# Filler products of the identity in the planned idle of TensorE, and the conditioning padded to 128 columns

## Chip, cores and metric

The kernel runs on one core of a Trainium2 chip. The metric is device time in microseconds; the time before is the median of three runs, 1363.4 us (1363.39 to 1395.84).

## What is computed

Sixteen sequences `b` of 256 positions and 256 channels pass through two blocks, all in float32. The reference, cut:

```python
m = silu(cond) @ w_ada + b_ada            # cond is [16, 256]; nine chunks of 256 columns
h = _ln(x) * (1 + sc_msa) + sh_msa
x = x + self_attn(h) * g_msa              # 16 heads, rolled windows of 128
h = _ln(x) * (1 + sc_mca) + sh_mca
x = x + topk_cross_attn(h, ctx) * g_mca   # the 16 largest scores of each row are kept
h = _ln(x) * (1 + sc_mlp) + sh_mlp
x = x + swiglu(h) * g_mlp
...
# second block: _ada_ln of x and of ctx with silu(cond) @ Wss + bss, then cross attention
return x_q + (out @ Wp + bp)
```

Every shift and scale is thus a product of a 256-column slice of `w_ada` or `Wss` with the conditioning of all 16 sequences. It is made once, near the start, and used for all of them.

## The kernel before

All work is declared through `plan.op(engine, cost, emit, reads, writes, ...)`. `Plan.order()` sorts the operations by a due time from the table `DUE` (in units of one sequence) and their number, and that is the order in which every engine's instructions are written out. No cost enters the sort. `order()` then walks this list with the planned costs (`cost`, `hold`, `SWITCH`, `LAG`, and for DMAs `ISSUE`, `BEGIN`, `LAND`, `RATE`, `OPEN`) and gives each operation a planned start and end. This walk decides one thing in the program: which of the equal buffers of a kind (eight PSUM banks of the kind `W`, five `prT`, and so on) an operation takes, namely the one that the walk sees free first. `run()` then calls each operation's `emit` in that order.

TensorE's steps that matter here, by the line of the matmul:

- `ada_columns` (L703): for one shift or scale, four calls of `matmul` with a 128x128 slice of weights as the stationary operand and `condT[:, c, :]`, 16 columns, as the moving one. A float32 call makes two MATMUL records (a transpose makes one), so this is eight records. There are ten such operations, two for each of five norms; they are planned at 1.7 us each. `conditioned` makes `condT` (DVE L688), `out_of_it` (DVE L709, L711) adds the bias.
- `gate_rows` (L744): `condT[:, c, :]` as the stationary operand, 256 moving columns.
- `product` (L475), `values` (L511), `projected` (L558) and the feed-forward (L888, L915): 256 moving columns, 128x128 stationary.
- `four` (L780 and L788 for self attention, L827 for the top-k scores, L932 and L944 for the last attention): four calls that sit in the four groups of 32 rows. L827 has 512 moving columns in each call.
- `weighted` (L581): probabilities times values, in the four groups of 32 columns. `turned` (L449) and `probs_turned` (L525): transposes.

A top-k round is L827, then for each of its four banks on VectorE `MAX8` (L846), two `MATCH_REPLACE8` (L854), `MAX8` (L866) and two more `MATCH_REPLACE8` (L871); ScalarE makes the exponentials (L859), GpSimd multiplies (L875), TensorE transposes the product (L525). `self_attention` puts its row maxima into `q2` by sixteen tiny DMAs on SP's queue (`lower`, L605, eight for each half of the heads) before L788 runs. After each residual add GpSimd and VectorE normalize (L399, L425 to L437), TensorE turns (L449), and the next product follows.

The order of the start: sequence 0's self attention (planned and run up to about 50 us), its normalization and query product, its first top-k round, into which sequence 1's self attention and the rest of the weights are worked; from sequence 2 on, the stages of three sequences interleave. The last sequence is worked in two halves of 128 positions, with little beside them.

## Time and profile before

| | |
|---|---|
| median of the runs | 1363.4 us |
| the profiled execution's own time | 1365.2 us |
| its span, first to last instruction | 1363.1 us |
| mean granted TensorE clock | 0.981 |
| busy: TensorE, VectorE, GpSimd, ScalarE | 1327.1, 1216.9, 1026.4, 1014.4 us |
| chain that ended last, TensorE's share | 87% |

A timeline row gives start, duration from the first start to the last end of the merged instructions, engine, line, operation, shapes and count; in brackets stands the engine's idle time before it and what released it. The length of a run of matmuls is better read from its start to the next row's start, since the last one's drain overlaps what follows. The clock of a stretch is the granted share of TensorE's full rate.

### The profile page before, as it was taken

To read this page: it belongs to the slowest core of one execution; us is meant where nothing else is said; L and a number is where in the kernel's file an instruction comes from. 1 tells how busy PE (TensorE), PEld (TensorE's weight loads), DVE (VectorE), ACT (ScalarE), POOL (GpSimd) and SP (SyncE) were. 2 spreads that over 40 slices of the span, in tenths; PEclk is the share of its full clock that TensorE was granted. 3 is DMA by queue.
4 is the path that set the end of the run, shared out by engine and by line. 5 is a ranking of instruction groups with operands and counts; after the bars stand their busy time and mean duration, and the time that the engine had idled before them with its cause. 6 is when DMAs were issued, how large, how long until landed. Compare 5 with 4: busy or idle time off the path is not lost.

```text
span 1363.1 us, 38514 instructions
## 1 busy us (share of the span) xinstructions
PE 1327.1 (97%) x13464; PEld 1040.8 (76%) x13464; DVE 1216.9 (89%) x4357; ACT 1014.4 (74%) x2359; POOL 1026.4 (75%) x1552
## 2 busy tenths in 40 slices
PE   8699999999999999999999999999999999999996
PEld 6466787878778787877878787787878777787875
DVE  3699999999999999999999999999999999998734
ACT  4256778877777878777787878778787877877773
POOL 2456887878788787878878787787878787878752
PEclk9788999999999999999999999999999999999998
DMA  5412000101000010100001010001101000000000
GB/s 158 147 53 58 18 25 18 40 18 41 16 20 25 19 40 18 41 17 18 25 22 37 17 41 18 18 25 22 36 18 41 25 18 25 26 2 10 10 2 18
DMA packets 64161, 42.44 MB, mean 31 GB/s; under 512 B 37764, under 2 KB 56752, under 8 KB 63712
## 3 DMA queue, kind: packets, MB, share of 16 engines
q1 hardware_dynamic: 63967, 39.99, 10.9%
q8 instruction: 107, 1.75, 0.5%
q14 instruction: 87, 0.70, 0.2%
HBM read 35.14 MB, written 4.29 MB: 29 GB/s over the span
## 4 chain that ended last, share of the span: by engine, by line
PE 87%; DVE 5%; POOL 2%; DMA 2%; SPq 1%; issue 1%; ACT 1%; ACTq 0%; POOLq 0%; DVEq 0%
PE W L888 17%; PE W L475 11%; PE W L581 11%; PE W L525 8%; PE W L915 7%; PE W L511 6%; PE W L558 6%; PE W L944 5%; PE W L932 5%; PE W L827 5%; PE W L449 3%; PE W L788 3%; PE W L780 2%; DVE rest L854 1%; DVE rest L871 1%
## 5 line engine op out<-in xcount | busy, mean ns | idle before, releaser
L875 POOL TENSOR_TENSOR prT<-rest,prT 128x512 f32<-128x512 f32 x256 | 325.7, 1273 | 63.5 <-DVE rest L871 49.8
L859 ACT ACTIVATE prT<-W,ntop 128x256 f32<-128x256 f32 x512 | 216.8, 510 | 76.0 <-POOL ntop L848 64.3
L588 DVE TENSOR_REDUCE nm<-W 128x2 f32<-128x512 f32 (+1 forms) x384 | 236.9, 681 | 28.1 <-PE W L932 16.0
L888 PE MATMUL W<-xT,w_L_xcond_w_m 128*128 128x256 f32 (+1 forms) x1088 | 249.0, 375 | 1.5 <-ACT xT L463 1.5
L612 ACT ACTIVATE pTO<-W 128x512 f32<-128x512 f32 (+1 forms) x392 | 200.5, 613 | 62.0 <-PE W L944 37.6
L888 PEld LDWEIGHTS W<-xT,w_L_xcond_w_m 128*128 128x128 f32 x1088 | 189.1, 190 | 57.0 <-ACT pTO L612 10.9
L854 DVE MATCH_REPLACE8 rest<-top,W 128x256 f32<-128x256 f32 x512 | 208.2, 416 | 0.2 <-issue 0.2
L871 DVE MATCH_REPLACE8 rest<-top,rest 128x256 f32<-128x256 f32 x512 | 205.5, 409 | 0.0
L846 DVE MAX8 top<-W 128x8 f32<-128x256 f32 x512 | 187.0, 417 | 14.7 <-PE W L827 14.5
L866 DVE MAX8 top<-rest 128x8 f32<-128x256 f32 x512 | 187.3, 410 | 0.0
L525 PE MATMUL W<-ident,prT 128*128 128x128 f32 x1024 | 144.4, 279 | 11.1 <-POOL prT L875 11.1
L528 ACT ACTIVATE pTT<-W 128x512 f32<-128x512 f32 x256 | 148.4, 621 | 8.8 <-PE W L525 8.7
L541 POOL TENSOR_TENSOR on<-tr,rec 128x128 f32<-128x128 f32 (+1 forms) x162 | 71.0, 443 | 98.6 <-DVE rec L540 98.2
L525 PEld LDWEIGHTS W<-ident,prT 128*128 128x128 f32 x1024 | 120.3, 143 | 32.6 <-POOL prT L875 14.6
L905 POOL TENSOR_TENSOR mb<-ma,mb 128x256 f32<-128x256 f32 (+1 forms) x136 | 94.7, 697 | 62.7 <-ACT mb L903 50.6
L538 DVE STREAM_TRANSPOSE tr<-W 128x256 f32<-128x256 f32 (+1 forms) x162 | 79.2, 490 | 48.1 <-PE W L581 40.1
L915 PE MATMUL W<-w_L_xcond_w_m,h 128*128 128x256 f32 x512 | 113.8, 380 | 0.0
L581 PE MATMUL W<-pTO,v 128*32 128x128 f32 (+1 forms) x2112 | 108.1, 329 | 2.3 <-ACT pTO L612 2.0
L915 PEld LDWEIGHTS W<-w_L_xcond_w_m,h 128*128 128x128 f32 x512 | 95.9, 190 | 13.6 <-POOL prT L875 0.8
L908 POOL TENSOR_TENSOR h<-h,mb 128x256 f32<-128x256 f32 (+1 forms) x136 | 94.8, 697 | 8.3
L581 PEld LDWEIGHTS W<-pTO,v 128*32 128x32 f32 x2112 | 57.8, 111 | 42.6 <-ACT h L907 10.2
L903 ACT ACTIVATE mb<-W,half 128x256 f32<-128x256 f32 (+1 forms) x136 | 69.6, 513 | 9.7 <-PE W L888 8.4
(126 smaller groups left out, 2675.2 us busy)
## 6 DMA issues: line engine op xcount, KB each, us to landing
gate<-gates SPq DMA_DIRECT2D x48, 256.0 KB
q<-nmT SPq DMA_DIRECT2D x480, 1.0 KB
cx<-in_ctx_dram SPq DMA_DIRECT2D x19, 256.0 KB
cx<-in_ctx_dram SPq DMA_DIRECT2D x104, 32.0 KB
rest<-in_L_xcond_w_ada_dram SPq DMA_DIRECT2D x9, 256.0 KB
x<-in_x_dram SPq DMA_DIRECT2D x16, 128.0 KB
x<-in_x_dram SPq DMA_DIRECT2D x32, 64.0 KB
w_L_xcond_w_m<-in_L_xcond_w_m_dram SPq DMA_DIRECT2D x1, 2048.0 KB
```

Source lines behind the costliest of these rows:

```text
L525: nc.tensor.transpose(w.t[:, ts(n, P)], flat[:, ts(n, P)], ident)
L581: nc.tensor.matmul(po.t[ds(NW * j, NW), ds(q0, nq)], v.t[:, kt, 8 * m + 2 * j + a, :], pT.t.rearrange("p n q -> p (n q)")[:, ds(part, nq)] ...
L588: op("DVE", 0.61, lambda j=j, s=s: nc.vector.tensor_reduce(nm.t[:, k, ds(j, groups, step=4)], s.t.rearrange("p (g k) -> p g k", g=groups), ...
L612: op("ACT", 0.24 + q * 0.0005, lambda s=s, pT=pT: nc.scalar.activation(pT.t.rearrange("p n q -> p (n q)")[:, :q], s.t[:, :q], AF.Exp), r=[ ...
L846: nc.vector.max(top.t[:, a, 0:8], s.t[:, ts(a, L)])
L854: nc.vector.match_replace(rest.t[:, a, :], top.t[:, a, 0:8], s.t[:, ts(a, L)], TAKEN)
L859: nc.scalar.activation(pr.t[:, a, :], s.t[:, ts(a, L)], AF.Exp, bias=ntop.t[:, a:a + 1])
L866: nc.vector.max(top.t[:, a, 8:16], rest.t[:, a, :])
L871: nc.vector.match_replace(rest.t[:, a, :], top.t[:, a, 8:16], rest.t[:, a, :], TAKEN)
L875: op("POOL", 1.25, lambda: nc.gpsimd.tensor_tensor(pr.t, rest.t, pr.t, ALU.mult), r=[rest, pr], w=[pr])
L888: nc.tensor.matmul(w.t[:, :q], w_m1.t[:, c, ds(n0, P)], xT.t[:, c, :q], start=c == 0, stop=c == NCC - 1)
L915: nc.tensor.matmul(pp.t[:, ts(k, C)], hs[f].t[:, ts(k, P)], w_m2.t[:, f, :], start=f == 0, stop=f == NHC - 1)
```

## The change

`order()` looks at every TensorE operation whose planned start is more than `IDLE` = 0.8 us after the planned end of the one before it. If a PSUM bank was free by that end plus 0.3 us, it notes `n = int((gap - 0.3) / FILLER)` fillers, with `FILLER` = 0.43 us, for the bank freed last among these, and books the bank until the operation starts. `run()` writes the fillers out just ahead of the operation. A filler is a float32 matmul of the 128x128 identity with the identity repeated four times, 512 moving columns, whose result nobody reads. Two planned DMA constants change, `ISSUE` from 0.47 to 0.53 and `LAND` from 1.0 to 0.4.

`condT` becomes 128 columns for each of its two chunks, the last 112 zero (one memset), and `ada_columns` multiplies all 128 and uses the first 16; it is now planned at 0.9 us instead of 1.7. `gate_rows` takes the first 16 columns as before.

```diff
-ISSUE, BEGIN, LAND, RATE, OPEN = 0.47, 0.9, 1.0, 320.0, 8
+
+IDLE, FILLER = 0.8, 0.43
+ISSUE, BEGIN, LAND, RATE, OPEN = 0.53, 0.9, 0.4, 320.0, 8
...
             o.start = t
+            if o.eng == "PE" and t - free["PE"] > IDLE and free["PE"]:
+
+                n = int((t - free["PE"] - 0.3) / FILLER)
+                ok = [z for z in slots["W"] if z[0] < free["PE"] + 0.3]
+                if ok and n:
+                    at, slot = ok[-1]
+                    slots["W"].remove((at, slot))
+                    insort(slots["W"], (t, slot))
+                    o.fill = self.tiles["W"][slot], n
...
+            if o.fill:
+                self.filler(*o.fill)
             o.emit()
...
+    def filler(t, n):
+        for _ in range(n):
+            nc.tensor.matmul(t, ident, ident.unsqueeze(1).to_broadcast([P, 4, P]), start=True, stop=True)
+    plan.filler = filler
...
-    condT = fixed("condT", [P, NCC, B])
+    condT = fixed("condT", [P, NCC, P])
+    nc.vector.memset(condT.t, 0.0)
...
-        op("DVE", 0.2, lambda: nc.vector.tensor_copy(condT.t.rearrange("p c b -> p (c b)"), w.t[:, :NCC * B]), r=[w], w=[condT])
+        op("DVE", 0.2, lambda: nc.vector.tensor_copy(condT.t[:, :, :B], w.t[:, :NCC * B].rearrange("p (c b) -> p c b", c=NCC)), r=[w], w=[condT])
...
-                    nc.tensor.matmul(pm.t[:, ts(m, B)], w.t[:, c, ts(m, P)], condT.t[:, c, :], start=c == 0, stop=c == NCC - 1)
-        op("PE", 1.7, emit, r=[w, condT], w=[pm], mode=128)
+                    nc.tensor.matmul(pm.t[:, ts(m, P)], w.t[:, c, ts(m, P)], condT.t[:, c, :], start=c == 0, stop=c == NCC - 1)
+        op("PE", 0.9, emit, r=[w, condT], w=[pm], mode=128)
...
-                nc.tensor.matmul(pg.t[:B, :C], condT.t[:, c, :], w.t[:, c, :], start=c == 0, stop=c == NCC - 1)
+                nc.tensor.matmul(pg.t[:B, :C], condT.t[:, c, :B], w.t[:, c, :], start=c == 0, stop=c == NCC - 1)
```

The two lines of `out_of_it` read `pm.t[:, ds(m * P, B)]` instead of `pm.t[:, ts(m, B)]`.

More of the change, by code (lines that the diff above doesn't have):

```diff
@@ L181 @@
 class Op:
-    __slots__ = ("tag", "eng", "cost", "hold", "own", "kb", "emit", "due", "mode", "takes", "uses", "after", "start", "end", "n")
+    __slots__ = ("tag", "eng", "cost", "hold", "own", "kb", "emit", "due", "mode", "takes", "uses", "after", "start", "end", "n", "fill")
 class Plan:
@@ L200, in op @@
         o.eng, o.cost, o.emit, o.mode, o.n = eng, cost, emit, mode, len(self.ops)
-        o.tag = self.tag
+        o.tag, o.fill = self.tag, None
         o.after, o.takes, o.uses = {*after}, [], []
@@ L708, in out_of_it @@
                 if plus_one:
-                    nc.vector.tensor_scalar(dst.t[:, m, :], pm.t[:, ts(m, B)], col(bias, chunk + m), 1.0, ALU.add, ALU.add)
+                    nc.vector.tensor_scalar(dst.t[:, m, :], pm.t[:, ds(m * P, B)], col(bias, chunk + m), 1.0, ALU.add, ALU.add)
                 else:
-                    nc.vector.tensor_scalar(dst.t[:, m, :], pm.t[:, ts(m, B)], col(bias, chunk + m), None, ALU.add)
+                    nc.vector.tensor_scalar(dst.t[:, m, :], pm.t[:, ds(m * P, B)], col(bias, chunk + m), None, ALU.add)
         op("DVE", 0.32, out_of_it, r=[pm, cols(bias)], w=[dst])
```

## Prediction

> **What bounds the kernel now.** I read the page first: the busy shares, and the row of granted clock.

> ```profile
> span 1363.1 us, 38514 instructions
> ...
> PE 1327.1 (97%) x13464; PEld 1040.8 (76%) x13464; DVE 1216.9 (89%) x4357; ACT 1014.4 (74%) x2359; POOL 1026.4 (75%) x1552
> ...
> PEclk9788999999999999999999999999999999999998
> ```

> TensorE (PE) sets the pace; from about 140 us to 1280 us it is never idle and at full clock, and VectorE (DVE) is close behind. What this change can touch lies in the first three or four slices of 34 us and in the last two. So next the busy time by stretch, TensorE alone (columns: stretch and its length, busy time with count, granted clock, DMA share, GB/s).

> ```profile
> 31.00:32.00 1.00, 0.64 (x24) 1.00 0.15 33
> 32.00:33.00 1.00, 1.00 (x16) 0.71 0.02 2
> 40.00:44.00 4.00, 4.00 (x65) 0.50 1.01 290
> 46.00:47.00 1.00, 1.00 (x5) 0.96 0.97 385
> ...
> 62.00:64.00 2.00, 0.00 (x0) 0.79 0.03 6
> 74.00:78.00 4.00, 4.00 (x33) 0.50 0.02 6
> 80.00:81.00 1.00, 1.00 (x26) 0.89 0.00 0
> 98.00:100.00 2.00, 1.27 (x9) 1.00 0.04 13
> 100.00:102.00 2.00, 0.93 (x4) 0.67 0.59 166
> ```

> The clock falls to half three times: from 32.4 to 46.1, 63.2 to 80.2 and 100.7 to 110.9 us. It also reads 0.66 in two stretches of 5 us near the end (1335 to 1340, 1345 to 1350). Then the timeline of TensorE, and of VectorE, where the longest idle lies:

> ```profile
> 58.24 1.14 PE L827 MATMUL W<-k,q 32*128 32x512 f32 x8 [0.56 <-ACT q L486]
> 68.24 1.11 PE L525 MATMUL W<-ident,prT 128*128 128x128 f32 x4 [8.86 <-POOL prT L875]
> 69.29 2.09 PE L827 MATMUL W<-k,q 32*128 32x512 f32 x8
> 71.31 1.11 PE L525 MATMUL W<-ident,prT 128*128 128x128 f32 x4
> ...
> 84.65 1.14 PE L827 MATMUL W<-k,q 32*128 32x512 f32 x8
> 85.72 1.08 PE L581 MATMUL W<-pTO,v 128*32 128x128 f32 x32
> ```

> ```profile
> 69.57 0.75 DVE L866 MAX8 top<-rest 128x8 f32<-128x256 f32 x2
> 71.39 0.77 DVE L846 MAX8 top<-W 128x8 f32<-128x256 f32 x2 [1.08 <-PE W L827]
> ```

> TensorE waits 8.86 us for the first transposed probabilities while VectorE works off four banks; VectorE itself is out of work at 70.3 us and waits for the second L827. So here VectorE is the bound, and L827's place in TensorE's order feeds it.

> **What a filler costs.** The nearest rows: 16 records of 256 columns (L475) run from 23.99 to 27.44 us, 3.45 us, or 0.216 us a record and 0.43 us a call. A 512-column call has twice the columns: 0.86 us. L827 has 512 columns; its four calls sit beside each other in four row groups and take 85.72 - 84.65 = 1.07 us, some 0.2 of it for the change of mode, which leaves 0.87 for calls of that length. The planned 0.43 is therefore half. At half clock the first L475 records (16 in 5.14 us from 12.09, part cold) and L511 (8 in 3.49 us from 76.86, 0.87 a call of 256) give 1.7 us a filler. I take 0.86 with the clock up; 0.43 and 1.7 are the ends.

> **How many fillers, and where.** This is a count from the walk in `order()`, with the new constants put in by hand; the plan's times are not used as times. Gaps over 0.8 us with a bank free:

> - before the second L703, gap 1.07: 1; before the first L475 (waits for w_qkv), 1.77: 3;
> - the shorter L703 opens gaps before the first L788 (1.03: 1), before both L581 of sequence 0 (1.39: 2, 1.31: 2) and before the L449 of prep0 (1.51: 2); before the first L827, 1.13: 1;
> - before the L525 at 68.24, 9.01: 20;
> - in the end: before two L888 (1.20: 2, 1.33: 2), an L475 (1.20: 2), an L932 (1.18: 2), an L944 (0.90: 1), an L581 (1.34: 2) and the last L558 (1.89: 3).

> At the short gaps from 63.9 to 110 and at 1213 all banks are taken, so nothing goes in. That is 32 in front and 14 at the end, 46 calls or 92 records. No other engine's order, and no DMA of SP's queue or GpSimd's, is added or moved, since the sort knows no cost; buffers may rotate differently, which I put at nothing (bound 1 us either way).

> **Part by part.**

> *Padding.* Ten L703 steps of eight records. With 16 columns they take 0.92 us at full clock (49.00 to 49.92) and 1.73 cold (4.43 to 6.16): the weight loads set the pace (LDWEIGHTS 128x128, median 192 ns, overlapped). 128 columns stream in half of 0.216 us, 0.11 a record, 0.86 for eight. So padding costs nothing in itself (bound 0 to 0.2 us each, 2 in all). The memset of 256 columns lies in VectorE's idle ahead of 2.92 us (1.78 us, waiting for a DMA): nothing, 0.3 if that cover were gone. What it may bring is clock: in the 3.4 us before 32.4 TensorE ran 1.0 us of L703, two short L788 and only 0.36 us idle, and still fell to half. With 16 of 128 columns counted as work the rest was about 1.8 us; the stretch from 56.3 to 59.7 had 2.4 us and kept the clock. Padded it would be 2.8. I take it as kept.

> [...]

> *0 to 30 us.* The filler ahead of the second L703 (cold, 1.7 us for 0.2 idle) and three ahead of L475 (2.6 us for 1.6 idle) push L475 from 12.09 to about 14.5; having started warm it needs 3.45 instead of 5.3 us. Net +0.5 (+4 if the clock is still low then, -1 if neither waits).

> *30 to 58 us.* At full clock L788, L703, L581, L780 and L744 would save up to 6.8 us (13.6 us at half rate). SP's sixteen L605 (issued 25.5 to 35.6 at about 0.6 us) still hold the second L788 back to about 36.6, against 36.20 now, and ScalarE's four exponentials (2.06 us) follow; GpSimd's chain holds L558 to about 44.3 against 46.11. So -2, less 0.3 for the two fillers ahead of L449 and one ahead of L827: L827 ends near 57.6 instead of 59.4, -1.8 (bounds -3 and +3, the fillers without the clock).

> *58 to 140 us.* Twenty fillers last 17.2 us, from 57.6 to 74.8, where the probabilities are ready near 66.4. They write the bank whose reader (ACT q L486) is done, so they wait for nothing. L525 and the second L827 are behind them; L827 ends at 76.4 instead of 71.4. VectorE starts its second round +5.0 late: its 13 us of cover end 6.6 us too early. After that TensorE is at full clock where it was at half, which removes VectorE's 1.15 us wait for L581 at 81.56 and part of its 2.7 us idle from 110 to 140. TensorE's own balance is no worse (it has 7.9 us of cold loss and 6 us of idle to give from 71 to 140), but VectorE is busy over 90% there. Of +5 I leave +2 at 140 us; bounds -3 (TensorE's balance alone decides) and +7 (VectorE recovers nothing and the clock still dips at 100).

> *140 to 1280 us.* No filler, TensorE full, so the +2 is carried.

> *End.* The rows of the idle, each filler run charged by 0.86 less the idle there:

> ```profile
> 1307.88 3.07 PE L888 MATMUL W<-xT,w_L_xcond_w_m 128*128 128x128 f32 x24 [0.93 <-ACT xT L463]
> ...
> 1334.96 1.28 PE L475 MATMUL W<-xT,w_L_xcond_Wq 128*128 128x128 f32 x8 [0.55 <-ACT xT L463]
> 1336.79 3.44 PE L932 MATMUL W<-k,q 32*128 32x256 f32 x32 [0.55 <-ACT q L497]
> ```

> Two fillers are 1.7 us: +1.2 and +0.8 at the two L888 (idle 0.55 at 1291 and 0.93), +1.2 at L475, +1.2 at L932, +0.5 at L944, +0.4 at the last L581, which ScalarE holds anyway, +1.0 at the last L558 (2.6 us against 1.11 idle and a first half that had already run). All are on the chain of waits, and nothing after makes it good. The two stretches at 0.66 cost 3.4 us of TensorE; I take 1 us back. Sum +5 (bounds +2, +7).

> **Sum.** +2 and +5 give +7 on the span of 1363.1. The profiled execution took 1365.2 us, 2.1 over its span and 1.8 over the median; on the median this is 1363.4 + 7 = 1370.

> [...]

> **Rivals.**

> 1. *The excess is absorbed.* TensorE's balance, not VectorE's late start, carries to 140 us: +6.6 at L525, less 4.4 and 3.9 of cold time and 0.8 of idle, is -2.5; with +2 at the end, 1363, and down to 1356 if the end costs nothing. For it: TensorE has 87% of the chain. Against it: the chain from 59 to 95 us runs over VectorE.
> 2. *A filler does take 0.43 us.* Then 8.6 us fit into 8.86, VectorE's waits of 1.1 and 1.15 us go, front -4, end -2: 1357. Against it: every row of columns above.
> 3. *Slower by over 2%: products of the identity don't hold the clock.* Then fillers 5 to 20 of the long gap take 1.7 us, some 14 us more, and VectorE's second round starts 19 late; with little recovered, +17, and 12 for the fourteen at the end, +3 in front: 1395. It decides once the long run lasts about 30 us. For it: the clock fell amid short, narrow matmuls; against: these are full, dense 128x128 products.

> **How the numbers follow.** My forecast 0.60 (its own range 1363 to 1379); rival 1 0.24 (1355 to 1365); rival 2 0.06; rival 3 0.06; 0.04 for anything else. The range 1355 to 1382 leaves out rival 3, half of rival 2 and the edges of the others, under 2 in 10. A measurement of this kernel can tell about 2% from no change, that is below 1336 or above 1391: faster 0.02, slower 0.06 (rival 3), same 0.92.

> **What would show it.** Right: 92 records more on TensorE, each filler row near 0.43 us a record; L525 of the first round 6 to 7 us after its probabilities are ready; a VectorE wait of some 8 us for the second L827; the clock at 1.00 from 30 to 100. Wrong: fillers in 0.22 us a record (rival 2), a clock of 0.50 beside fillers (rival 3), an L703 still followed by half clock (padding does nothing, +2), or VectorE's lag gone by 140 us (rival 1).

## The result, and the profile after

The changed kernel takes 1374.1 us (median of four runs, 1373.2 to 1374.82), the one before 1363.39 beside it: a ratio of 1.0084, 95% interval 1.0066 to 1.0101. (Ratios here compare the means of the runs in the fast state, so the run of 1395.84 us is not in this one.) It is 11 us slower, clear of the noise but within the 2%; the forecast was 1370 in a range of 1355 to 1382. The profiled execution took 1373.99 us over a span of 1371.6.

The first lines of the page and its row of granted clock (lines after the change stand 18 or 19 lower: L846 is the old L827, L543 the old L525, L599 the old L581, L493 the old L475, L467 the old L449; L354 is the filler):

```profile
span 1371.6 us, 38691 instructions
...
PE 1348.6 (98%) x13556; PEld 1045.1 (76%) x13556; DVE 1217.0 (89%) x4358; ACT 1014.1 (74%) x2359; POOL 1025.5 (75%) x1552
...
PEclk9999999999999999999999999999999999999999
```

TensorE has 92 records more, as 46 calls make, and its clock is now up nearly everywhere (0.996 on the mean, 0.981 before). The kernel is slower all the same. Where, TensorE's and then VectorE's timeline show:

```profile
49.62 1.88 PE L354 MATMUL W<-ident 128*128 128x512 f32 x4
...
55.67 1.13 PE L354 MATMUL W<-ident 128*128 128x512 f32 x2 [0.70 <-DVE nm L606]
56.73 1.14 PE L846 MATMUL W<-k,q 32*128 32x512 f32 x8
57.80 17.43 PE L354 MATMUL W<-ident 128*128 128x512 f32 x40
75.07 0.60 PE L543 MATMUL W<-ident,prT 128*128 128x128 f32 x4
75.60 1.14 PE L846 MATMUL W<-k,q 32*128 32x512 f32 x8
```

```profile
68.06 0.74 DVE L885 MAX8 top<-rest 128x8 f32<-128x256 f32 x2
76.76 0.76 DVE L865 MAX8 top<-W 128x8 f32<-128x256 f32 x2 [7.96 <-PE W L846]
```

The twenty fillers last from 57.80 to 75.07, 17.27 us or 0.86 each, where the idle before was 8.86. The second top-k product stands behind them, and VectorE, which waited 1.08 us for it, waits 7.96 and starts its second round at 76.76 instead of 71.39 us.

At the end of the run, TensorE again:

```profile
1340.49 1.88 PE L354 MATMUL W<-ident 128*128 128x512 f32 x4
1342.21 1.05 PE L493 MATMUL W<-xT,w_L_xcond_Wq 128*128 128x128 f32 x8
1343.10 1.88 PE L354 MATMUL W<-ident 128*128 128x512 f32 x4
1344.91 2.01 PE L951 MATMUL W<-k,q 32*128 32x256 f32 x32
...
1363.79 2.84 PE L354 MATMUL W<-ident 128*128 128x512 f32 x6
1366.47 1.03 PE L576 MATMUL W<-w_L_xcond_Wp,oT 128*128 128x256 f32 x4
```

Each of the two pairs shown fills 1.7 us where 0.55 was idle. The two halves of L951 take 2.01 instead of 3.44 us, at full clock now (1.00 from 1342 to 1371 us), which gives part of it back. The last run of three alone holds the last product from 1363.8 to 1366.5.

### The profile page after: what moved, and what is told of

Same layout as the page of the kernel before. It is cut to its first block, busy times and chain, and to the rows that moved or that the text cites. A ratio compares the mean times of both kernels' runs of the same rounds, so it can differ in the third digit from the quotient of the medians.

```text
span 1371.6 us, 38691 instructions
## 1 busy us (share of the span) xinstructions
PE 1348.6 (98%) x13556; PEld 1045.1 (76%) x13556; DVE 1217.0 (89%) x4358; ACT 1014.1 (74%) x2359; POOL 1025.5 (75%) x1552
## 3 DMA queue, kind: packets, MB, share of 16 engines
q8 instruction: 108, 1.77, 0.6%
## 4 chain that ended last, share of the span: by engine, by line
PE 91%; DVE 4%; ACT 2%; DMA 1%; issue 1%; POOL 1%; SPq 0%; DVEq 0%; ACTq 0%; POOLq 0%
PE W L907 17%; PE W L493 12%; PE W L599 11%; PE W L934 8%; PE W L543 8%; PE W L529 6%; PE W L576 6%; PE W L846 5%; PE W L963 5%; PE W L951 4%; PE W L354 3%; PE W L467 3%; PE W L807 3%; PE W L799 2%; DVE rest L873 1%; DVE nm L606 1%
## 5 line engine op out<-in xcount | busy, mean ns | idle before, releaser
L894 POOL TENSOR_TENSOR prT<-rest,prT 128x512 f32<-128x512 f32 x256 | 325.8, 1274 | 63.2 <-DVE rest L890 50.5
L878 ACT ACTIVATE prT<-W,ntop 128x256 f32<-128x256 f32 x512 | 216.5, 510 | 76.7 <-POOL ntop L867 67.3
L606 DVE TENSOR_REDUCE nm<-W 128x2 f32<-128x512 f32 (+1 forms) x384 | 236.7, 678 | 27.3 <-PE W L951 17.8
L865 DVE MAX8 top<-W 128x8 f32<-128x256 f32 x512 | 186.3, 414 | 22.5 <-PE W L846 22.4
L543 PE MATMUL W<-ident,prT 128*128 128x128 f32 x1024 | 142.3, 276 | 3.6 <-POOL prT L894 2.9
L924 POOL TENSOR_TENSOR mb<-ma,mb 128x256 f32<-128x256 f32 (+1 forms) x136 | 94.8, 698 | 63.2 <-ACT mb L922 51.2
L543 PEld LDWEIGHTS W<-ident,prT 128*128 128x128 f32 x1024 | 119.0, 142 | 23.9 <-POOL prT L894 4.8
L599 PE MATMUL W<-pTO,v 128*32 128x128 f32 (+1 forms) x2112 | 104.7, 325 | 2.1 <-ACT pTO L630 2.0
L934 PEld LDWEIGHTS W<-w_L_xcond_w_m,h 128*128 128x128 f32 x512 | 95.9, 190 | 13.7 <-POOL prT L894 0.8
L599 PEld LDWEIGHTS W<-pTO,v 128*32 128x32 f32 x2112 | 55.9, 109 | 42.9 <-ACT h L926 9.4
L917 ACT ACTIVATE h<-W,half 128x256 f32<-128x256 f32 (+1 forms) x136 | 68.1, 501 | 12.9 <-PE W L907 12.8
```

Source lines behind the costliest of these rows:

```text
L543: nc.tensor.transpose(w.t[:, ts(n, P)], flat[:, ts(n, P)], ident)
L599: nc.tensor.matmul(po.t[ds(NW * j, NW), ds(q0, nq)], v.t[:, kt, 8 * m + 2 * j + a, :], pT.t.rearrange("p n q -> p (n q)")[:, ds(part, nq)] ...
L606: op("DVE", 0.61, lambda j=j, s=s: nc.vector.tensor_reduce(nm.t[:, k, ds(j, groups, step=4)], s.t.rearrange("p (g k) -> p g k", g=groups), ...
L865: nc.vector.max(top.t[:, a, 0:8], s.t[:, ts(a, L)])
L878: nc.scalar.activation(pr.t[:, a, :], s.t[:, ts(a, L)], AF.Exp, bias=ntop.t[:, a:a + 1])
L894: op("POOL", 1.25, lambda: nc.gpsimd.tensor_tensor(pr.t, rest.t, pr.t, ALU.mult), r=[rest, pr], w=[pr])
```

## The experiments

The theory was that the fillers are right in place but twice as long as planned, that VectorE's late second round is what costs in front, and that padding keeps the clock from 32 us on. The rivals: the excess is absorbed before 140 us; the loss comes from buffers or from the number of fillers; padding does nothing. Every kernel below computes the whole reference. Ratios are to the kernel before, with their 95% intervals; its median in these runs was 1363.3 to 1363.7 us.

**e1, padding alone.**

```diff
-IDLE, FILLER = 0.8, 0.43
+IDLE, FILLER = 1e9, 0.43
```

> The changed kernel without any filler; the padding and the two DMA constants stay. Theory (the fillers' excess over the idle is what costs; the padding alone keeps the clock up from 30 to 58 us): the first L846 ends 1.5 to 2.5 us earlier than the 59.4 of before, the clock stays at 1.00 from 32 to 46 us, the 8.9 us idle is back and the clock falls there as before; 1360 to 1362 us, 2 us under before. Rival (padding does nothing, the fillers between the L722 and L599 held the clock): 0.50 from 32 to 46 us, 1363. Second rival (the new constants turn the buffers in a worse order and that is part of the loss): over 1366.

Measured: 1360.16 us, ratio 0.9978 (0.9967 to 0.9990). The clock stays at 1.00 from 30 to 57 us and falls in the long idle as before (0.50 from 60 to 74 us). So without fillers the change is a small gain: the loss belongs to the fillers.

**e2, fillers alone.** The lines that write and read `condT` and its products go back with it.

```diff
-    condT = fixed("condT", [P, NCC, P])
+    condT = fixed("condT", [P, NCC, B])
...
-        op("PE", 0.9, emit, r=[w, condT], w=[pm], mode=128)
+        op("PE", 1.7, emit, r=[w, condT], w=[pm], mode=128)
```

> The changed kernel with the conditioning back at 16 columns, planned at 1.7 us. The walk then writes 36 fillers instead of 46: 2 before the first qkv product, 1 before the first L827-like top-k product, 20 in the long run, 13 at the end and none at the L581-like steps. Theory: the clock falls at 32 us as before, so the first top-k product ends near 59.4 to 60 instead of 57.8 and all later steps carry this; 1375 to 1377. Rival (the clock from 32 us is not worth anything, since SP's small DMAs hold that stretch): 1374, as the changed kernel.

Measured: 1372.63 us, ratio 1.0072 (1.0057 to 1.0087). The clock does fall, but only from 32.9 to 36.3 us, and the first top-k product ends at 56.92, sooner than in the changed kernel (57.80): of the twelve fillers ahead of it only three are left, since the longer plan of the conditioning's products leaves fewer gaps. My 1375 to 1377 was wrong. With fillers of this length the padded kernel is no faster than the unpadded one, but it also has ten fillers more.

**e3, half the fillers.**

```diff
-IDLE, FILLER = 0.8, 0.43
+IDLE, FILLER = 0.8, 0.86
```

> FILLER = 0.86 instead of 0.43, nothing else: 21 fillers instead of 46 (1, 1, 1, 1 in front, 10 in the long run of some 8.6 us, one each at six places at the end). Theory (VectorE's late second round is the cost): the second top-k product is done when VectorE runs out of work, near 69 us, instead of 76.7; VectorE restarts 2 us sooner than in before and finds TensorE at full clock; at the end one filler fits the idle. 1356 to 1361, faster than before by 2 to 7. Rival (whatever TensorE does there, VectorE's round and TensorE's full load after 140 us set the rest): 1362 to 1365, no better than before.

Measured: 1358.43 us, ratio 0.9961 (0.9948 to 0.9973). TensorE's timeline shows ten fillers that fit:

```profile
55.17 8.85 PE L354 MATMUL W<-ident 128*128 128x512 f32 x20
64.86 0.66 PE L543 MATMUL W<-ident,prT 128*128 128x128 f32 x4 [0.84 <-POOL prT L894]
65.45 1.14 PE L846 MATMUL W<-k,q 32*128 32x512 f32 x8
```

TensorE still waits 0.84 us for the probabilities, the second top-k product is there at 66.5, and VectorE goes from its first round into the second at 66.85 with no wait. The theory holds.

**e4, without the long run.**

```diff
-                if ok and n:
+                if ok and 0 < n < 10:
```

> The changed kernel without the run of 20; the other 26 fillers stay. Theory: VectorE restarts at about 69.7 us (before 71.4, changed 76.8); the clock falls in the idle as before; the 5.1 us that the changed kernel carries from there on are gone and 1 to 2 gained, the end still costs 3.4: 1365 to 1367. Rival (the run's delay is paid back by the clock it keeps, and the loss arises elsewhere): 1372 to 1376.

Measured: 1366.83 us, ratio 1.0023 (1.0014 to 1.0032), 7.3 under the changed kernel. VectorE restarts at 70.58. The run of twenty is two thirds of the loss.

**e5, without the fillers at the end.**

```diff
-                if ok and n:
+                if ok and n and t < 1000:
```

> The changed kernel without the 13 fillers after 1280 us; the 33 in front stay. Theory: the end takes again what it takes before (81.7 us from the L581 near 1281 to the last instruction, changed 85.2), the 5 us of the front stay: 1369 to 1371. Rival (the fillers at the end win back by the clock what they add there, and the profile's 3.4 us is that one execution's): 1373 to 1375.

Measured: 1369.9 us, ratio 1.0048 (1.0036 to 1.0061): 4.2 us less than the changed kernel, and in its profile the end takes 81.9 us again. The thirteen at the end cost about four.

**e6, narrow products in the long run** of the half-count kernel.

```diff
+        if n == 10:
+            for _ in range(38):
+                nc.tensor.matmul(t[:, :B], ident, ident[:, :B], start=True, stop=True)
+            return
```

> The half-count kernel with its run of 10 fillers of 512 columns replaced by 38 products of the identity with 16 of its columns, about as long (8 x 0.115 us a record pair is 0.23 us a call, 8.7 us). Theory (streamed columns, not the number of instructions or the absence of idle, hold the clock): the clock falls to 0.50 some 4 to 7 us into the run, the narrow calls then take twice as long, and the second top-k product is late: 1361 to 1366. Rival (any busy TensorE holds the clock): 1.00 throughout and 1358, as the half-count kernel.

Measured: 1364.56 us, ratio 1.0007 (0.9998 to 1.0016); all of e3's gain is gone. Busy time by stretch, TensorE alone:

```profile
56.00:58.00 2.00, 2.00 (x21) 1.00 0.75 210
58.00:60.00 2.00, 2.00 (x15) 0.70 0.04 11
60.00:64.00 4.00, 4.00 (x21) 0.50 0.29 69
```

TensorE is busy without a break, by its records, and its clock falls to half 4.3 us into the run, as in the idle of before (at 63.2 us, 3.8 after the last product). The 38 calls last 12.4 us (54.51 to 66.89) instead of the 8.7 expected. The wide products of e3 held the clock (1.00 from 56 to 64 us) and narrow ones, just as busy (4.00 of 4 us in both from 60 to 64), did not: in these two runs the clock went with the streamed columns, 512 a record against 16, not with the number of records, 20 against 76.

**e7, the two DMA constants alone** (e1's edit and e2's together).

> The kernel before with only the two new DMA constants. They change no instruction and no order, only which of the equal buffers an operation takes. Theory: 1362.5 to 1364, no difference. Rival (the rotation of the buffers is worth 1 us or more either way): outside of that.

Measured: 1362.1 us, ratio 0.9996 (0.9987 to 1.0004). The interval includes no difference, so putting the buffers' rotation at nothing was near enough; the median is 1.6 us under that of before, a little below my range, and the rival's 1 us is not excluded. Between 30 and 57 us the clock of its profile dips from 34.7 to 38.2 us only.

**e8, half the fillers and no padding** (e2's edit and e3's together).

> FILLER = 0.86 and the conditioning at 16 columns again: 17 fillers (1 ahead of the first qkv product, 10 in the long run, 6 at the end), against 21 of the padded one. Theory (padding keeps the clock from 32 us on and is worth 1 to 2 us): 1359.5 to 1361. Rival (with the start warmed by one filler the padding is worth nothing, as the run with fillers and no padding hinted): 1357 to 1359.

Measured: 1357.53 us, ratio 0.9958 (0.9945 to 0.9972), the fastest kernel here. It can't be told from e3, which has the padding, and it kept 1.00 from 30 to 46 us without it:

```profile
32.00:36.00 4.00, 3.27 (x58) 1.00 0.03 6
36.00:40.00 4.00, 3.83 (x60) 1.00 0.67 214
```

**e9, all 46 calls, half as wide.**

```diff
-            nc.tensor.matmul(t, ident, ident.unsqueeze(1).to_broadcast([P, 4, P]), start=True, stop=True)
+            nc.tensor.matmul(t[:, :2 * P], ident, ident.unsqueeze(1).to_broadcast([P, 2, P]), start=True, stop=True)
```

> The changed kernel with fillers of 256 columns instead of 512; all 46 calls stay where they are. Theory (the filler's length against the planned 0.43 is the whole fault): 0.43 us a call, the run of 20 lasts 8.6 us, VectorE has no wait for the second top-k product, and the end costs nothing: 1356 to 1360. Rival (the number of fillers or the places they stand in cost by themselves): over 1362.

Measured: 1359.43 us, ratio 0.9975 (0.9966 to 0.9985). The run of twenty lasts 8.93 us (55.52 to 64.45), VectorE starts its second round at 66.43 without a wait, and the end takes 81.6 us, as in before. With the length that the plan assumes, the same number in the same places gains: the length was the fault. One place is not free even so, that ahead of the first top-k product: its filler waits 1.22 us for the last reader of its bank, and the start of the product comes 1.3 us later behind the query product (L493) than in e3, which has no filler there.

**e10, fourteen instead of twenty.**

```diff
+                n = min(n, 14)
                 if ok and n:
```

> The changed kernel with the long run cut from 20 to 14 fillers (12.1 us instead of 17.3). Theory (VectorE's restart is carried one for one to the end, no part of it is absorbed): VectorE waits 2.8 us instead of 8.0 for the second top-k product, and the time is 5.2 us below the changed kernel's 1374.1: 1368 to 1370. Rival (a part is absorbed while VectorE is not yet the bound, as I had predicted with 2 of 5 left): 1371 to 1373.

Measured: 1368.35 us, ratio 1.0045 (1.0031 to 1.0058). VectorE's row (the lines of this kernel stand one lower: L866 is L865, L847 is L846):

```profile
71.19 0.76 DVE L866 MAX8 top<-W 128x8 f32<-128x256 f32 x2 [2.81 <-PE W L847]
```

Its wait is 5.15 us shorter and the time 5.75 us: nothing is absorbed, against the rival's 1371 to 1373.

**e11, the kernel before once more.** No edit, one profiled execution.

> The kernel before, unchanged, for a second profile. Theory (where the clock falls after 30 us depends on how the activity windows happen to lie in one execution, since the unpadded kernel with fillers that fit kept 1.00 there): another pattern than 0.50 from 32.4 to 46.1 us, the first top-k product ending at 57 to 59.4. Rival (the narrow product always drops it there): again 0.50 from about 32 to 46.

Measured: 1363.38 us, span 1361.4. TensorE by stretch:

```profile
32.00:36.00 4.00, 4.00 (x52) 0.58 0.03 6
36.00:40.00 4.00, 4.00 (x42) 0.50 0.66 160
40.00:46.00 6.00, 6.00 (x75) 0.76 0.93 275
```

The clock falls at 32.6 us again but is back three microseconds sooner, and the first top-k product starts at 56.91 instead of 58.24. So the rival is half right: the narrow product tends to drop it there (four of the six profiles with it); how long it stays down differs from one execution to the next (13.7 us in the first profile of before, 10.2 here). The theory's other pattern is there; that windows of activity make it, no run shows.

**e12, e8 without its six fillers at the end** (e5's edit on e8).

> The half-count, unpadded kernel with its 11 fillers in front and none of its six at the end. Theory (a filler that fits the idle gains only where it keeps the clock for work on the chain; at the end that is under 1 us): 1357.5 to 1359. Rival (they gain 2 or more): over 1359.5; or they cost: under 1357.

Measured: 1358.96 us, ratio 0.9969 (0.9957 to 0.9981); e8's interval overlaps it, so the times alone can't tell the two apart. From one product shortly before the end's fillers (the one of the table below) to the last instruction the profiles show 80.7 to 81.0 us in the three kernels with one filler at each place (e3, e6, e8) and 81.7 to 82.4 in the six with none (before, e1, e5, e7, e11, e12). One filler each at the end gains about 1 us.

## Why the prediction held, step by step

The number lies in the range, and the mechanism was the one forecast: VectorE's second round starts late, and the fillers at the end lie on the chain of waits. One step failed all the same, the recovery between 58 and 140 us, and its error of +3 is partly cancelled by an end that cost less than I took.

**What a filler costs: right.** 0.86 us (17.27 for twenty), from the rows of 256 and 512 columns. **How many: right**, 92 records; one of them stands at 137 us and not at the L944 where I had it. **Padding itself: right** at nothing: 0.99 us for its eight records (29.29 to 30.28) against 1.00 before (29.44 to 30.44), and 1.87 against 1.73 for the cold first one.

**0 to 30 us: -0.15 instead of +0.5**; the qkv product, L493, ran from 13.63 to 17.08, warm. That profile hides what the warm start is worth. Over all kernels the first L780, two steps on, starts at 19.1 to 20.7 us without fillers (before, e1, e7, e11), at 18.0 to 19.3 with the three long ones ahead of L493 (changed, e4, e5, e10), and at 17.4 to 18.2 with one (e3, e6, e8, e12), one profile each.

**30 to 58 us: the sum was near, by luck.** The first top-k product started 1.51 us sooner than in the profile of before, against my 1.8. Two terms were too small and nearly cancel. I compare the time from the start of the first L780 to that of the first L827. The profile of before needed 39.2 us, with 13.7 us of half clock; its second one (e11) 37.8. The kernels without the filler just ahead of L827, with a short dip or none, need 35.9 (e3, e6, e7, e8, e12; 36.1 in e1), padded or not. So the long dip of that one profile was worth 3.3 us, where I took 2. TensorE's products alone don't set this stretch when the clock is up: in e8, at 1.00 from 30 to 46 us, TensorE is busy for 14.55 of these 16 us and twice waits for SP's small DMAs (0.55 us ahead of 30.84 and 0.56 ahead of 35.95, `<-DMA q<-nmT`). The fillers cost 1.7 to 2.3 us there (37.6 in e5, 37.8 in the changed kernel, 38.2 in e4 and e10), where I took 0.3. Most of it is the single one ahead of L827: it waits for the last reader of its bank (0.70 us in the changed kernel, `<-DVE nm L606` in its row above, 0.43 to 1.22 in the six kernels that have it), and the product starts 0.9 to 1.5 us later for it. I had excluded such a wait for the long run and not looked for it here. As to the padding, whose 2.8 us of counted work were my estimate and are shown by no run: between 30 and 57 us the clock fell in four of the six unpadded profiles (before, e11, e7, e2, not in e8 and e12) and in none of the eight padded ones. Removing that dip was worth between nothing and 3.3 us.

**58 to 140 us: this step failed.** VectorE's restart, the first `MAX8` of its second round, was 5.4 us late, as I had said (5.0), after a wait of 7.96 (8). But I left 2 of the 5, since TensorE would be warm and VectorE had idle to give. To see what is left of the 5, I follow the time from the restart to one and the same product of the last sequence, its third L581 step on `pTT`; in before and in the changed kernel:

```profile
1281.39 1.08 PE L581 MATMUL W<-pTT,v 128*32 128x128 f32 x32
```

```profile
1286.44 1.08 PE L599 MATMUL W<-pTT,v 128*32 128x128 f32 x32
```

Every kernel needs nearly the same time from its restart to that product, wherever the restart lies (all in us; the last column is how much of that time the clock was at half):

| kernel | VectorE's restart | that product | between | at half clock |
|---|---|---|---|---|
| e12 | 65.6 | 1273.3 | 1207.6 | 6.8 |
| e9 | 66.4 | 1276.3 | 1209.8 | 10.2 |
| e8 | 66.8 | 1274.4 | 1207.7 | 6.8 |
| e3 | 66.9 | 1276.2 | 1209.4 | 10.2 |
| e7 | 69.4 | 1278.2 | 1208.8 | 13.2 |
| e6 | 70.0 | 1281.0 | 1211.0 | 19.5 |
| before, second profile (e11) | 70.1 | 1278.9 | 1208.9 | 13.8 |
| e1 | 70.2 | 1278.8 | 1208.6 | 12.9 |
| e4 | 70.6 | 1279.9 | 1209.3 | 4.5 |
| e10 | 71.2 | 1279.7 | 1208.5 | 3.4 |
| before | 71.4 | 1281.4 | 1210.0 | 19.1 |
| e5 | 75.6 | 1285.6 | 1210.0 | 10.2 |
| e2 | 75.9 | 1283.9 | 1208.0 | 6.8 |
| changed | 76.8 | 1286.4 | 1209.7 | 10.2 |

The restart moves by 11 us, the time behind it by 3.4, and it is no shorter where the restart is late: nothing of the lateness is won back. VectorE did not use the idle that I had counted on. From the restart to 140 us it is busy for 63.91 of 68.60 us in before and for 59.65 of 63.20 in the changed kernel, 93 and 94%; from there to 1280 us TensorE is busy for 1138.71 of 1140 us in before.

The cold stretches that I counted as TensorE's reserve, at half of their length, were worth little. The two profiles with the most half clock (before and e6, over 19 us) need 1210.0 and 1211.0 us, the five with the least (3.4 to 6.8) 1207.6 to 1209.3: some 2 us where half of the difference in length would be 7. With one profile for each kernel that is a hint and not more. Nor does the clock stay at 1.00 to 100 us, which was one of my signs of being right. In the changed kernel TensorE idles again beside a VectorE that never does, and its clock falls:

```profile
80.00:84.00 4.00, 3.69 (x25) 2.99 (x19) 4.00 (x19) 3.07 (x7) 3.08 (x3) 0.63 0.01 2
...
107.00:114.00 7.00, 5.11 (x45) 3.36 (x44) 7.00 (x32) 4.25 (x10) 6.57 (x11) 0.60 0.01 3
```

(Columns after the stretch: busy TensorE, its weight loads, VectorE, ScalarE, GpSimd, then clock, DMA share, GB/s.) VectorE is busy 4.00 of 4 and 7.00 of 7 there.

**End: +3.4 in the profile (85.2 us from that product to the last instruction, 81.7 before), +4.2 by e5, against +5.** The mechanism was right and the sum a little high. The filler that I had put at the L944 (+0.5) is not there, and L951 alone gives back 1.4 us by the clock (1.94 us to the next row's start instead of 3.36), where I took 1 for all. All four profiles with the thirteen long fillers (changed, e2, e4, e10) need 85.2 to 86.5 us here.

**Sum.** +2 and +5 were to be +5.0 and +3.4: +8.5 on the span. On the medians it is 10.7, since the profiled execution of before (1365.2 us) had a longer dip than most: its mean clock is 0.981, and of the 21 runs of before beside e1 those at 0.981 took 1365.2 to 1366.2 us, those at 0.991 1359.9 to 1361.1. Against the second profile of before (span 1361.4) the changed span is 10.2 longer. Rival 1 (absorbed) falls by the table and by e10, rival 2 (0.43 us a filler) by the timeline, rival 3 (half clock beside fillers) too: 1.00 throughout the run of twenty. What rival 3 described is in e6, for narrow products (0.50 from 4.3 us into the run).

What stays open: whether padding together with fillers that fit is worth anything (e3 and e8 differ by less than their spread), and what makes the spread in the table beyond the half clock.

## What to carry to other kernels

Time put into an idle engine is free only as long as what stands behind it in that engine's order isn't what another engine is about to run out of: look for that engine's next wait, not for the idle. Fill less than the idle, and price the filler by rows of the same kernel, by its records and their columns; here half the number turned +0.8% into -0.4%. A clock that is low beside another engine's bound was little reserve here: over 19 us of half clock went with some 2 us.
